# Linear attention in a sandwich kernel: the output projection multiplied into the heads' sums, queries divided before it, and two stages of a state-space block moved from PSUM to SBUF

## The chip, the core and the metric

The kernel runs on one core of a Trainium2 chip. The core has five engines with queues of their own: TensorE (PE: matmuls, with the loads of stationary operands listed as PEld), VectorE (DVE), ScalarE (ACT), GpSimd (POOL) and SyncE (SP), which here issues nearly all DMAs. Each works through its instructions in the order in which they were emitted, and waits on semaphores for what the others have produced. Matmuls write into PSUM; VectorE and ScalarE take the results from there. All data are fp32.

The metric is the device time of one launch in microseconds. Three runs of the kernel before gave 2832.69, 2833.66 and 2833.69 us: median 2833.66.

## The reference

4 sequences of 1024 tokens with 256 features go through four blocks in turn: an encoder of 4 layers, a LoRA mixture, a state-space (Mamba) block of 512 channels with 16 states each, and a mixture of 8 experts that take up to 320 tokens each. The change touches two places. In each encoder layer, with 16 heads of 16 features:

```python
qp = elu(q) + 1                      # tokens x heads x 16
kp = elu(k) + 1
kv   = einsum('bshd,bshm->bhmd', kp, v)      # per head, summed over the sequence
ksum = sum(kp, axis=1)
z    = 1 / (einsum('blhd,bhd->blh', qp, ksum) + 1e-6)
attn = einsum('blhd,bhmd,blh->blhm', qp, kv, z)
x = x + (attn.reshape(b, t, 256) @ Wo + bo)
```

In the state-space block, before the recurrence over time:

```python
xc = conv_b + sum_k xp[:, k:k+L, :] * conv_w[:, k]     # 4 taps
xc = silu(xc)
dt, Bm, Cm = split(xc @ W_x)
delta = softplus(dt @ W_dt + b_dt)
h = h * exp(delta * A) + delta * xc * Bm ;  y = sum over the states of h * Cm
```

## The kernel before

**Tiling.** Tokens are cut into 8 blocks of 512 (two to a sequence), and each block into four tiles of 128. One encoder layer on one block is a "unit": there are 32. The units of two sequences alternate in two lanes, and a unit's work is cut into steps: `a_norm`, `a_turn`, `a_query`, `a_keys`, `a_sums` (projections and the heads' sums), `b_heads`, `b_turn`, `b_out`, `b_turn2` (attention and its output), `f_up`, `f_down` (feed-forward), and after the last layer `c_*` (the LoRA mixture). The loop at the end of `layers` (L1648) runs over the units and places in each round the early steps of unit u+3, the sums of u+2, the attention of u+1 and the feed-forward of u side by side. Between these steps, `pump` (L1637) draws pieces of `stream`: for each block `front` (input projection, convolution, softplus), `scan` (the recurrence), `back` and `route`, and at the end the experts. What remains of `stream` after the last round follows without encoder work beside it.

**Order.** Nothing is emitted at once. Every call is recorded (`record`, L191) with its reads, its writes and a planned duration from small tables (L132 to L152: for instance `SCATTER`, the planned price of one scattering DMA on GpSimd, 1010). `order` (L289) then repeatedly picks the operation that can start first by the plan; of several, the one recorded first. So an edit moves instructions on all engines.

**Buffers.** A tag of a pool stands for a ring of equal tiles. A tile is given a slot when its first operation is picked, and within a tag slots are given in the order of recording (L302 to L306, L332 to L339): a tile cannot get a slot before the tile recorded ahead of it. Four rings matter here: `mm`, four PSUM tiles of 512 columns, which all products use except the heads' sums (`kv`), the scan's sums (`y`) and the scan's states (`h`, two tiles); `tok`, four tiles for token-major data; `qe`, two tiles of 512 columns; `hc`, nine tiles.

**Attention before the change.** `a_sums` adds up, for each half c of the features, kp^T against v and a column of ones, over both blocks of a sequence, in PSUM. After the second block VectorE multiplies by the head mask (zero outside the 16x16 blocks on the diagonal) into `kvm`, 17 columns per head, the last of which holds the sums of kp. `b_heads` (L751) multiplies each tile of 128 queries with `kvm`; VectorE adds the epsilon to the 17th columns, takes the reciprocal (`z`) and multiplies (`a`, a `tok` tile). `b_turn` transposes `a` on TensorE, eight 128x128 transposes, and ScalarE copies the result into an `hT` tile. `b_out` (L780) multiplies it with `wo` and adds to the residual `X`.

**State-space stages before the change.** In `front`, each of four channel groups has an input product in an `mm` tile `ps`. ScalarE copies it to `xi` and writes the last tap with the bias back into `ps`; VectorE adds the other three taps into `ps` (L1093), and ScalarE and VectorE take sigmoid and product from it. Later another product in an `mm` tile gives dt @ W_dt; ScalarE makes |x| and relu(x) of it (the latter back into the tile), then exp and log; VectorE and GpSimd correct the logarithm, VectorE adds the parts into the tile (L1141), ScalarE copies that to `du`, and VectorE multiplies by `xc`.

**The scan.** A group of four channel rows by two state halves gives eight tiles `hc` = h * C; when all four of a half are there, TensorE sums them over the states with `gsum` into `y` (`sums`, L1164). The sums of one group are recorded behind the first two products of the next.

Of the kernel before, what the change touches and what calls it, by code (L numbers as in the profile page):

```python
# [9 lines left out]
F32 = mybir.dt.float32  # L10
# [138 lines left out]
ISSUE, SCATTER, FIND = 350, 1010, 1500  # L149
# [237 lines left out]
def sandwich_kernel(ctx: ExitStack, tc: tile.TileContext, io: dict):  # L387
# [34 lines left out]
    nc.vector.memset(eps, LN_EPS)  # L422

# [118 lines left out]
    def layers(ctx: ExitStack):  # L542
# [28 lines left out]
        head_blocks = head_mask.rearrange("p (h m) -> p h m", m=HD)  # L571

# [142 lines left out]
        def a_sums(u):  # L715
            s, l, j = units[u]
            half = j % NB
            if half == 0:
                KV[s, l] = ps_kv.tile([P, NC_D, P + 1], F32, tag="kv", name="kv")
            acc, kv = KV[s, l], S[u].pop("kv")  # L720
            for c in range(NC_D):
                for i in range(NT):
                    nc.tensor.matmul(
                        acc[:, c, :],
                        kv[:, 0, i, c, 0:P],
                        kv[:, 1, i, c, :],
                        start=half == 0 and i == 0 and c == 0,
                        stop=half == NB - 1 and i == NT - 1 and c == NC_D - 1,
                        skip_group_check=True,
                    )  # L730
            if half == NB - 1:

                kvm = apool.tile([P, NC_D, HC, HD + 1], F32, tag="kvm", name="kvm")
                shape = [P, NC_D, HC, HD]
                nc.vector.tensor_tensor(
                    kvm[:, :, :, 0:HD],
                    acc[:, :, 0:P].rearrange("p c (h m) -> p c h m", h=HC),
                    head_blocks.unsqueeze(1).to_broadcast(shape),
                    ALU.mult,
                )  # L740
                nc.vector.tensor_tensor(
                    kvm[:, :, :, HD],
                    head_blocks[:, :, 0].unsqueeze(1).to_broadcast([P, NC_D, HC]),
                    acc[:, :, P : P + 1].to_broadcast([P, NC_D, HC]),
                    ALU.mult,
                )
                for k in range(NB):
                    S[u - k]["kvm"] = kvm


        def b_heads(u):  # L751
            j = units[u][2]
            qT, kvm = S[u].pop("qT"), S[u].pop("kvm")
            nc.gpsimd.tensor_tensor(X[j], X[j], over_tiles(weight(u)["ro"][:, 0, :]), ALU.add)
            a = tok("att")
            for i in range(NT):
                ps = mm([P, NC_D * HC, HD + 1], "psa")
                for c in range(NC_D):
                    nc.tensor.matmul(
                        ps[:, c * HC : (c + 1) * HC, :].rearrange("p h m -> p (h m)"),  # L760
                        qT[:, c, i * P : (i + 1) * P],
                        kvm[:, c, :, :].rearrange("p h m -> p (h m)"),
                        start=True,
                        stop=True,
                    )
                z = small.tile([P, NC_D * HC], F32, tag="z", name="z")
                nc.vector.tensor_scalar(z, ps[:, :, HD], ATTN_EPS, None, ALU.add)
                nc.vector.reciprocal(z, z)
                nc.vector.tensor_tensor(
                    a[:, i, :].rearrange("p (h m) -> p h m", m=HD),  # L770
                    ps[:, :, 0:HD],
                    z.unsqueeze(2).to_broadcast([P, NC_D * HC, HD]),
                    ALU.mult,
                )
            S[u]["a"] = a

        def b_turn(u):
            S[u]["aT"] = turn(S[u].pop("a"))

        def b_out(u):  # L780
            j = units[u][2]
            w, aT = weight(u), S[u].pop("aT")
            for pr in range(NT // 2):
                ps = mm([P, 2, D], "pso")
                for k in range(2):
                    i = 2 * pr + k
                    for c in range(NC_D):
                        nc.tensor.matmul(
                            ps[:, k, :],
                            aT[:, c, i * P : (i + 1) * P],  # L790
                            w["wo"][:, c, :],
# [243 lines left out]
        def front(j):  # L1035
# [43 lines left out]
            for db, ps in project(w_in[0]):  # L1079
# [4 lines left out]
                else:  # L1084
                    nc.gpsimd.tensor_copy(xi[:, 0:3], m["hist"][:, db, :])
                nc.scalar.copy(xi[:, 3 : TB + 3], ps)
                nc.scalar.activation(
                    ps, ps, AF.Identity, bias=mcol[:, db, M_CB : M_CB + 1], scale=w[:, 3:4]
# [3 lines left out]
                for k in range(3):  # L1092
                    nc.vector.scalar_tensor_tensor(  # L1093
                        ps, xi[:, k : k + TB], w[:, k : k + 1], ps, ALU.mult, ALU.add
                    )
                s = sigmoid(ps)
                nc.vector.tensor_tensor(xc[:, db, :], s, ps, ALU.mult)
# [26 lines left out]
            for db in range(NDB):  # L1124
# [10 lines left out]
                nc.scalar.activation(ps, ps, AF.Relu, bias=bdt)  # L1135
# [5 lines left out]
                nc.vector.tensor_tensor(ps, v1, ps, ALU.add)  # L1141
                nc.scalar.copy(du[:, 0, :], ps)
                nc.vector.tensor_tensor(du[:, 1, :], xc[:, db, :], ps, ALU.mult)
# [4 lines left out]
        def scan(j):  # L1148
# [12 lines left out]
            for db in range(NDB):  # L1161
# [13 lines left out]
                for r in range(GQ):  # L1175
# [6 lines left out]
                    for q in range(4):  # L1182
# [10 lines left out]
                        for k in range(NSH):  # L1193
# [12 lines left out]
                            hc = tiles[q, k] = spool.tile([P, TB], F32, tag="hc", name="hc", bufs=9)  # L1206
# [441 lines left out]
        for u in range(-3, len(units) + 4):  # L1648
# [28 lines left out]
            parts.append(lambda: load(u + 2, "wo", "ro"))  # L1677
# [125 lines left out]
```

## Time and profile before

| | us |
|---|---|
| median of three runs | 2833.66 |
| the profiled execution | 2831.64 |
| its span, first to last instruction | 2829.7 |
| TensorE busy | 2424.3 |
| VectorE busy | 1876.2 |
| ScalarE busy | 1550.4 |
| GpSimd busy | 1122.1 |
| mean granted TensorE clock | 0.925 |

All lines of code that the planner emits carry one line number, L203, so groups are told apart by engine, operation, tile names and shape. A row of the groups reads: line, engine, operation, output tile <- inputs, shapes and count; then busy time in all and the mean length of one in ns; then how long the engine had been idle just before these instructions, and which engine's write to which tile ended that wait. Names are those of the tiles in PSUM or SBUF, not of the variables: `wo<-` groups contain the output projection, `t` is several things (weights and transposed blocks of the state-space part, `du`, small columns of the normalisation). An fp32 matmul stands as two records, a transpose as one. Means include the overlap of one instruction with the next; busy time doesn't.

Most of the scans run beside the encoder: at the encoder's last matmul, at 2296.6 us, the rows of `hc` show that about five and a half of the eight scans are done. The rest, with most of the experts, fills the last 533 us.

### The profile page before, as it was taken

The page shows a single profiled execution, that of the slowest core. Times are in us where ns is not written, and L with a number is a line of the kernel's source. Part 1 is how long each engine was busy: PE and PEld are TensorE (multiplying, and loading weights), DVE is VectorE, ACT ScalarE, POOL GpSimd, SP SyncE. Part 2 cuts the span into 40 slices and gives each one's busy share as a digit, 9 for nine tenths or more (in the row PEclk, how much of TensorE's full clock was granted, in tenths as well). Part 3 has the DMA queues.
Part 4 walks back from the last instruction along what each step waited for, and adds up shares of the span by engine and source line. Part 5 has one row for each costly group of instructions (what it writes and reads, how often), then busy time and mean ns, then how long its engine had stood idle before and what let it go on. Part 6 is the DMA issues. An engine that isn't in the chain of part 4 may idle for free. (4 is left out here: it accounts for less than half of the span.)

```text
span 2829.7 us, 30664 instructions
## 1 busy us (share of the span) xinstructions
PE 2424.3 (86%) x9172; PEld 1440.9 (51%) x9172; DVE 1876.2 (66%) x4182; ACT 1550.4 (55%) x3213; POOL 1122.1 (40%) x878
## 2 busy tenths in 40 slices
PE   4979799999899999997989999986986875789776
PEld 2556466666556555555645556543543443334343
DVE  3231323244387778885458979987987995599896
ACT  4333543545665666554665666665664544666443
POOL 0100011022054445452235446544654572467663
PEclk8989899999999999998999999998997886899878
DMA  4011110122253344442244445545445343867652
GB/s 116 17 56 48 52 38 28 40 71 82 96 182 125 104 137 144 127 134 66 92 152 137 145 131 173 165 139 168 135 144 157 108 151 112 248 185 216 189 163 62
DMA packets 202221, 342.09 MB, mean 121 GB/s; under 512 B 32197, under 2 KB 79514, under 8 KB 198976
## 3 DMA queue, kind: packets, MB, share of 16 engines
q1 hardware_dynamic: 197760, 334.80, 38.2%
q0 software_dynamic: 4288, 5.27, 1.0%
q8 instruction: 74, 1.21, 0.2%
q14 instruction: 99, 0.81, 0.1%
HBM read 281.13 MB, written 59.92 MB: 121 GB/s over the span
## 5 line engine op out<-in xcount | busy, mean ns | idle before, releaser
L203 POOL TENSOR_TENSOR dbu<-dd,bc 128x512 f32<-128x512 f32 x512 | 657.7, 1321 | 485.8 <-DVE h L203 262.2
L203 ACT ACTIVATE h<-dd,A 128x512 f32<-128x512 f32 x512 | 346.1, 687 | 340.1 <-DVE hc L203 333.0
L203 PE MATMUL mm<-w,fT 128*128 128x256 f32 x2176 | 486.6, 381 | 5.9 <-ACT t L203 3.3
L203 PEld LDWEIGHTS mm<-w,fT 128*128 128x128 f32 x2176 | 410.4, 190 | 84.6 <-issue 16.0
L203 PE MATMUL y<-hc,gsum 128*32 128x512 f32 x1024 | 260.4, 647 | 114.3 <-DVE hc L203 104.6
L203 DVE TENSOR_TENSOR hc<-h,bc 128x512 f32<-128x512 f32 x512 | 343.0, 679 | 21.0 <-PE y L203 17.5
L203 DVE TENSOR_TENSOR_SCAN h<-h,last_h,dbu 128x512 f32<-128x512 f32 x256 | 322.3, 1277 | 39.0 <-ACT h L203 31.5
L203 DVE TENSOR_TENSOR_SCAN h<-h,dbu 128x512 f32<-128x512 f32 x256 | 306.1, 1218 | 33.1 <-ACT h L203 26.0
L203 POOL TENSOR_TENSOR X<-X,ro 128x1024 f32<-128x1024 f32 x64 | 150.3, 2354 | 420.4 <-ACT tok L203 388.2
L203 PE MATMUL mm<-hT,w1a 128*128 128x512 f32 (+1 forms) x576 | 268.4, 614 | 9.1 <-ACT hT L203 8.2
L203 PE MATMUL mm<-hT,w1b 128*128 128x512 f32 (+1 forms) x576 | 253.3, 592 | 9.8 <-DVE tok L203 8.5
L203 ACT ACTIVATE fT<-mm,cols 128x512 f32<-128x512 f32 x256 | 172.3, 680 | 128.8 <-PE mm L203 127.8
L203 PE MATMUL mm<-wkv,hT 128*128 128x512 f32 x512 | 228.7, 599 | 4.5 <-DVE xc L203 3.2
L203 PE MATMUL mm<-ident,tok 128*128 128x128 f32 x952 | 145.0, 298 | 90.4 <-ACT tok L203 84.6
L203 DVE TENSOR_TENSOR X<-X,mm 128x512 f32<-128x512 f32 x128 | 86.8, 680 | 189.1 <-PE mm L203 188.8
L203 PEld LDWEIGHTS mm<-ident,tok 128*128 128x128 f32 x952 | 116.1, 152 | 157.2 <-ACT tok L203 88.6
L203 PEld LDWEIGHTS mm<-hT,w1a 128*128 128x128 f32 x576 | 111.8, 204 | 142.4 <-issue 99.3
L203 PEld LDWEIGHTS mm<-hT,w1b 128*128 128x128 f32 x576 | 110.3, 195 | 140.8 <-issue 106.9
L203 ACT ACTIVATE tok<-X,nb,rs 128x256 f32<-128x256 f32 x288 | 149.3, 589 | 34.1 <-DVE nb L203 33.8
L203 PEld LDWEIGHTS y<-hc,gsum 128*32 128x32 f32 x1024 | 38.8, 111 | 243.6 <-DVE hc L203 166.2
L203 PEld LDWEIGHTS mm<-wkv,hT 128*128 128x128 f32 x512 | 97.5, 192 | 122.0 <-issue 105.1
L203 ACT ACTIVATE tok<-tok,nb,rs 128x256 f32<-128x256 f32 x252 | 131.1, 590 | 38.1 <-DVE nb L203 34.4
(184 smaller groups left out, 3710.9 us busy)
## 6 DMA issues: line engine op xcount, KB each, us to landing
dd<-dud SPq DMA_DIRECT2D x512, 256.0 KB
w<-in_w_dram SPq DMA_DIRECT2D x16, 1024.0 KB
dud<-t SPq DMA_DIRECT2D x32, 512.0 KB
tok<-in_x_dram SPq DMA_DIRECT2D x16, 512.0 KB
wkv<-in_wkv_dram SPq DMA_DIRECT2D x16, 512.0 KB
w1a<-in_w_dram SPq DMA_DIRECT2D x16, 512.0 KB
w1b<-in_w_dram SPq DMA_DIRECT2D x16, 512.0 KB
t<-in_w_in_dram SPq DMA_DIRECT2D x16, 512.0 KB
```

What stands on the lines that cost most here:

```text
L203: getattr(getattr(self.nc, engine), name)(*map(put, args), **{k: put(v) for k, v in kwargs.items()})
```

## The change

In the attention, `kvm` keeps only the masked sums (`a_fold`). A second tile, `den`, holds the sums of kp, spread over the 16 columns of their head. `a_fold2` transposes the masked sums, and `a_fold3` multiplies them by `wo` once per sequence and layer, which gives `kvo`, 256x256. `b_heads` multiplies `den` with the queries, so that each feature row holds its head's denominator for 512 tokens; ScalarE takes logarithm and exponential of minus that, and VectorE multiplies the queries by it in place. `b_out` multiplies the divided queries by `kvo`. `b_turn` and `att` are gone. The tiles of the fold and the divisors `z` take the ring `qe`; `den` and `kvo` have one buffer each. The loads of `wo` come one unit earlier.

In `front`, the convolution is added up in `xc` in SBUF, from the first tap on; softplus's positive part goes to a `qe` tile, and the sum goes straight into `du` without ScalarE's copy. The ring `hc` gets eight tiles, and the planned price of a scatter is 1700.

```diff
-ISSUE, SCATTER, FIND = 350, 1010, 1500
+ISSUE, SCATTER, FIND = 350, 1700, 1500
...
-            if half == NB - 1:
-                kvm = apool.tile([P, NC_D, HC, HD + 1], F32, tag="kvm", name="kvm")
...
+        def a_fold(u):
+            s, l, j = units[u]
+            if j % NB < NB - 1:
+                return
+            acc = KV.pop((s, l))
+            t = apool.tile([P, 2, NC_D, P], F32, tag="qe", name="kvm")
+            nc.vector.tensor_tensor(
+                t[:, 0], acc[:, :, 0:P], head_mask.unsqueeze(1).to_broadcast([P, NC_D, P]), ALU.mult
+            )
+            den = apool.tile([P, NC_D, P], F32, tag="den", name="den", bufs=1)
+            nc.vector.tensor_tensor(
+                den,
+                head_mask.unsqueeze(1).to_broadcast([P, NC_D, P]),
+                acc[:, :, P : P + 1].to_broadcast([P, NC_D, P]),
+                ALU.mult,
+            )
...
+        def a_fold2(u):
...
+            pt = mm([P, NC_D, P], "ptk")
+            for c in range(NC_D):
+                nc.tensor.transpose(pt[:, c, :], t[:, 0, c, :], ident)
+            nc.scalar.copy(t[:, 1], pt)
+        def a_fold3(u):
...
+            ps = mm([P, NC_D, D], "psm")
+            for c in range(NC_D):
+                nc.tensor.matmul(
+                    ps[:, c, :], t[:, 1, c, :], weight(u)["wo"][:, c, :], start=True, stop=True
                 )
+            kvo = apool.tile([P, NC_D, D], F32, tag="kvo", name="kvo", bufs=1)
+            nc.scalar.copy(kvo, ps)
...
         def b_heads(u):
...
-            a = tok("att")
-            for i in range(NT):
-                ps = mm([P, NC_D * HC, HD + 1], "psa")
...
-                z = small.tile([P, NC_D * HC], F32, tag="z", name="z")
-                nc.vector.tensor_scalar(z, ps[:, :, HD], ATTN_EPS, None, ALU.add)
-                nc.vector.reciprocal(z, z)
...
-        def b_turn(u):
-            S[u]["aT"] = turn(S[u].pop("a"))
+            for c in range(NC_D):
+                ps = mm([P, TB], "psa")
+                nc.tensor.matmul(ps, den[:, c, :], qT[:, c, :], start=True, stop=True)
+                z = apool.tile([P, TB], F32, tag="qe", name="z")
+                nc.scalar.activation(z, ps, AF.Ln, bias=attn_eps)
+                nc.scalar.activation(z, z, AF.Exp, scale=-1.0)
+                nc.vector.tensor_tensor(qT[:, c, :], qT[:, c, :], z, ALU.mult)
...
-                            aT[:, c, i * P : (i + 1) * P],
-                            w["wo"][:, c, :],
+                            qT[:, c, i * P : (i + 1) * P],
+                            kvo[:, c, :],
...
+                t = xc[:, db, :]
                 nc.scalar.activation(
-                    ps, ps, AF.Identity, bias=mcol[:, db, M_CB : M_CB + 1], scale=w[:, 3:4]
+                    t, ps, AF.Identity, bias=mcol[:, db, M_CB : M_CB + 1], scale=w[:, 3:4]
                 )
...
-                        ps, xi[:, k : k + TB], w[:, k : k + 1], ps, ALU.mult, ALU.add
+                        t, xi[:, k : k + TB], w[:, k : k + 1], t, ALU.mult, ALU.add
                     )
-                s = sigmoid(ps)
-                nc.vector.tensor_tensor(xc[:, db, :], s, ps, ALU.mult)
+                s = sigmoid(t)
+                nc.vector.tensor_tensor(t, s, t, ALU.mult)
...
-                nc.scalar.activation(ps, ps, AF.Relu, bias=bdt)
+                r = apool.tile([P, TB], F32, tag="qe", name="over")
+                nc.scalar.activation(r, ps, AF.Relu, bias=bdt)
...
-                nc.vector.tensor_tensor(ps, v1, ps, ALU.add)
-                nc.scalar.copy(du[:, 0, :], ps)
-                nc.vector.tensor_tensor(du[:, 1, :], xc[:, db, :], ps, ALU.mult)
+                nc.vector.tensor_tensor(e, v1, r, ALU.add)
+                nc.vector.tensor_tensor(lv, xc[:, db, :], e, ALU.mult)
...
-                            hc = tiles[q, k] = spool.tile([P, TB], F32, tag="hc", name="hc", bufs=9)
+                            hc = tiles[q, k] = spool.tile([P, TB], F32, tag="hc", name="hc", bufs=8)
...
             add(a_sums, u + 2)
+            add(a_fold, u + 2)
             add(f_up, u, 0)
+            add(a_fold2, u + 2)
...
             add(b_heads, u + 1)
             add(f_up, u, 1)
+            add(a_fold3, u + 2)
...
-            add(b_turn, u + 1)
...
-            parts.append(lambda: load(u + 2, "wo", "ro"))
+            parts.append(lambda: load(u + 3, "wo"))
+            parts.append(lambda: load(u + 2, "ro"))
```

More of the change, by code (lines that the diff above doesn't have):

```diff
@@ L422, in sandwich_kernel @@
     nc.vector.memset(eps, LN_EPS)
+    attn_eps = cpool.tile([P, 1], F32, name="attn_eps")
+    nc.vector.memset(attn_eps, ATTN_EPS)
     nc = Program(tc)
@@ L570, in layers @@
                 units += [st and (st[0], st[1], st[0] * NB + k) for k in range(NB)]
-        head_blocks = head_mask.rearrange("p (h m) -> p h m", m=HD)
         W = {}
@@ L730, in a_sums @@
                     )
-            if half == NB - 1:
-                kvm = apool.tile([P, NC_D, HC, HD + 1], F32, tag="kvm", name="kvm")
[L734 to L739, printed above, removed]
-                )
[L741 to L748, printed above, removed]
+        def a_fold(u):
[14 more added lines that the diff above has]
+            )
+            S[u]["fold"] = t
+            for k in range(NB):
+                S[u - k]["den"] = den
@@ new lines, in a_fold2 @@
+        def a_fold2(u):
+            if "fold" not in S[u]:
+                return
+            t = S[u]["fold"]
+            pt = mm([P, NC_D, P], "ptk")
[3 more added lines that the diff above has]
+        def a_fold3(u):
+            if "fold" not in S[u]:
+                return
+            t = S[u].pop("fold")
+            ps = mm([P, NC_D, D], "psm")
+            for c in range(NC_D):
+                nc.tensor.matmul(
+                    ps[:, c, :], t[:, 1, c, :], weight(u)["wo"][:, c, :], start=True, stop=True
+                )
+            kvo = apool.tile([P, NC_D, D], F32, tag="kvo", name="kvo", bufs=1)
+            nc.scalar.copy(kvo, ps)
+            for k in range(NB):
+                S[u - k]["kvo"] = kvo
@@ L751, in b_heads @@
         def b_heads(u):
             j = units[u][2]
-            qT, kvm = S[u].pop("qT"), S[u].pop("kvm")
+            qT, den = S[u]["qT"], S[u].pop("den")
             nc.gpsimd.tensor_tensor(X[j], X[j], over_tiles(weight(u)["ro"][:, 0, :]), ALU.add)
-            a = tok("att")
-            for i in range(NT):
-                ps = mm([P, NC_D * HC, HD + 1], "psa")
[L758 to L765, printed above, removed]
-                z = small.tile([P, NC_D * HC], F32, tag="z", name="z")
-                nc.vector.tensor_scalar(z, ps[:, :, HD], ATTN_EPS, None, ALU.add)
-                nc.vector.reciprocal(z, z)
[L769 to L774, printed above, removed]
@@ L775, in b_heads @@
-            S[u]["a"] = a
-        def b_turn(u):
-            S[u]["aT"] = turn(S[u].pop("a"))
+            for c in range(NC_D):
[5 more added lines that the diff above has]
+                nc.vector.tensor_tensor(qT[:, c, :], qT[:, c, :], z, ALU.mult)
@@ L780, in b_out @@
         def b_out(u):
             j = units[u][2]
-            w, aT = weight(u), S[u].pop("aT")
+            w, qT, kvo = weight(u), S[u].pop("qT"), S[u].pop("kvo")
             for pr in range(NT // 2):
```

## The prediction

> **What bounds the kernel now.** I read the page's first parts, then busy times by stretch, then the groups of instructions kept apart by shape, with what ended the idle time before each. First the totals and the share of each fortieth of the span in tenths, from the page:
>
> ```profile
> PE 2424.3 (86%) x9172; PEld 1440.9 (51%) x9172; DVE 1876.2 (66%) x4182; ACT 1550.4 (55%) x3213; POOL 1122.1 (40%) x878
> ...
> PE   4979799999899999997989999986986875789776
> ...
> DVE  3231323244387778885458979987987995599896
> ```
>
> TensorE (PE) is near nine tenths for two thirds of the span; VectorE (DVE) joins it later. Busy times by stretch (length, then busy us and counts of PE, PEld, DVE, ACT, POOL, then granted clock, DMA share, GB/s):
>
> ```profile
> 0.00:700.00 700.00, 612.82 (x2312) 402.21 (x2313) 222.55 (x715) 317.06 (x717) 77.10 (x53) 0.94 0.18 54
> 700.00:1900.00 1200.00, 1107.68 (x4366) 668.96 (x4364) 894.90 (x1995) 739.40 (x1504) 538.29 (x423) 0.97 0.43 133
> 1900.00:2297.00 397.00, 310.81 (x1141) 169.63 (x1140) 340.94 (x666) 220.83 (x404) 218.94 (x175) 0.87 0.45 140
> 2297.00:2830.00 533.00, 393.04 (x1360) 200.10 (x1356) 417.82 (x808) 273.14 (x589) 287.77 (x229) 0.84 0.56 167
> ```
>
> The reader should see two regimes. Until 1900 TensorE is the bound: 613 of 700 us, then 1108 of 1200 us (92%), with VectorE at 32% and 75%. The last down-projection of the encoder ends at 2296.6 us in the timeline. Around it, from 1900, VectorE leads (341 of 397 us). The last 533 us are the remaining scans and the experts, which the change hardly touches. So what is taken from TensorE counts in the first two stretches. Third, the groups that the change removes, and idle time on TensorE ("idle" is before the group, with what ended it):
>
> ```profile
> L203 DVE TENSOR_TENSOR hc<-h,bc 128x512 f32<-128x512 f32 x512 | 343.0, 679 | 21.0 <-PE y L203 17.5 <-DMA bc<-bcd 1.6 <-DVE t L203 0.3
> ...
> L203 PE MATMUL mm<-hT,w1b 128*128 128x512 f32 x512 | 234.6, 612 | 9.8 <-DVE tok L203 8.5 <-ACT fT L203 1.2
> ...
> L203 PE MATMUL mm<-ident,tok 128*128 128x128 f32 x952 | 145.0, 298 | 90.4 <-ACT tok L203 84.6 <-DVE tok L203 2.8 <-DVE kv L203 1.7
> ...
> L203 PE MATMUL mm<-hT,wq 128*128 128x512 f32 x256 | 121.2, 618 | 4.7 <-ACT hT L203 3.5 <-DVE X L203 1.2
> L203 PE MATMUL mm<-wo,hT 128*128 128x256 f32 x512 | 118.8, 385 | 1.1 <-ACT hT L203 1.1
> ...
> L203 PE MATMUL mm<-kvm,qT 128*128 128x136 f32 x512 | 82.7, 311 | 40.7 <-ACT t L203 14.6 <-DVE tok L203 7.5 <-ACT fT L203 7.4
> ...
> L203 ACT ACTIVATE qe<-mm,nbq 128x512 f32<-128x512 f32 x64 | 43.4, 679 | 44.9 <-PE mm L203 44.2
> ...
> L203 ACT COPY hT<-mm 128x512 f32<-128x512 f32 x64 | 34.3, 584 | 23.3 <-PE mm L203 23.3
> ```
>
> A matmul that waits for a DVE or ACT instruction it takes no data from waits for one of the four PSUM tiles "mm": the heads' product (mm<-kvm,qT) waited 14.6 us for "ACT t", the copy that ends a softplus, and 7.5 us for "DVE tok", the division of the previous token tile.
>
> **What the Trainium skill says.** "Perfetto Trace Analysis", Optimization Strategy, says that repeating gaps on the engine that should be saturated can mean that no SBUF or PSUM buffer was free; the 14.6 us above agree. The same page, Optimizing Scalar/DVE Operations, prices a ScalarE access at about 93 ns in SBUF and 51 in PSUM, a VectorE access at 60 and 125. For ScalarE the trace agrees: the exponential of the sigmoid is 592 ns from PSUM and 630 from SBUF. For VectorE it doesn't show it: 128x512 products with a PSUM operand take 679 to 687 ns, one wholly in SBUF (tok with affine, 692). "VectorE: DVE Perf Modes", Why tensor_tensor can't do 2×_2P or 4×, leaves fp32 two-tensor operations no fast mode, and 692 ns for 512 columns agrees. So the convolution gains nothing per instruction by leaving PSUM.
>
> **The change part by part.** There are 32 units (block and layer) in 16 pairs. An fp32 matmul stands as two records, a transpose as one; I price by a group's busy time over its count, in which overlap is already taken out.
>
> 1. TensorE. Removed: the heads' products, 82.7 us, and the turning of their result, 8 transposes a unit, 256 of the 952 of "ident,tok": 256/952 x 145.0 = 39.0. Sum 121.7. Added: denominators, two 128x512 matmuls a unit, 128 records x 121.2/256 (row of wq) = 60.6; fold per pair two transposes, 32 x 145.0/952 = 4.9, and two 128x256 matmuls, 64 records x 118.8/512 (row of wo) = 14.8. Sum 80.3. The output projection keeps its shape and count. Net -41.4 us, 1.29 a unit.
> How much counts? The heads' products lie 192, 256 and 64 of 512 in the first three stretches: 12, 16 and 4 units, worth 15.5, 20.7 and 5.2 us. I take 0.95, 0.85 and 0.6 of these, by how far TensorE is the bound there: 14.7 + 17.6 + 3.1 = -35.4. Bounds: 0 where another engine takes over everywhere, -41.4.
>
> 2. VectorE. Removed: the three z groups (89.8 us in the view of tile z) and two masks (8.5). Added: the queries' division, 64 products of 128x512 at 680 ns = 43.5, and two 256-column masks a pair, 32 x 424 ns = 13.6. Net -41.2. That is what lets step 1 count where VectorE is nearly as busy; it isn't added again.
>
> 3. ScalarE. Removed: copies of the turned heads, 34.3, and the copy of delta into "du", 32 x 582 ns = 18.6. Added: logarithms, 64 x 679 (qe<-mm above) = 43.5; exponentials, 64 x 625 (qe<-qe in the same view) = 40.0; fold copies, 16 x (377 for 256 columns + 584 for 512) = 15.4. Net +46.0, 1.44 a unit. ScalarE is busy 739 of 1200 us in the second stretch, so most of it lies beside TensorE; but the scan waits for its exponential ("DVE h" for "ACT h", 57.5 us in the table of waits), and a queue in order gets later. I take +6 (a tenth of that). Bounds 0 and 20 units x 1.44 = +29.
>
> 4. PSUM freed at once. A convolution tile was held over two ScalarE and three VectorE operations, a sigmoid and a product; now over two ScalarE operations. A softplus tile was held over two GpSimd operations as well. The heads take two tiles a unit for one logarithm each, where four were held by VectorE, and their turn took two more. Idle ended by these releases: heads 14.6 + 7.5, w1b 8.5 (DVE tok), and from rows of the view not shown, input projection 3.5 and keys 3.2 (DVE xc), experts' transposes 9.4 (DVE t): 46.7 us. Some of it comes back as waiting for data. I take half, -23.4; bounds 0 and -46.7.
>
> 5. Ring "hc" from 9 to 8. One group of eight products fills it; the next group's first product must wait until the sums on TensorE have read the former. One element's time of slack is lost, 1.23 + 0.68 = 1.9 us. Now 17.5 of 21.0 us idle before hc are for "PE y". I take +8, near half as much again; bounds 0 and the slower rival below.
>
> 6. Buffers and queues. "qe" (two buffers) now also holds the folded sums, the divisors and softplus's positive part; queries stay until the output projection; "att" no longer takes a "tok" buffer or an "hT". The weights wo are fetched one unit earlier, since only the fold reads them: on SP's queue the scans' loads stand behind that fetch, and what it waits for now comes earlier. Net 0, plus or minus 8. The larger price of a scatter alters only the planned order on GpSimd. Its DMAs keep their count, 28 at 1012 and 24 at 1543 ns: 0, plus or minus 5. Start-up: from the mask at 71.8 to the first output projection at 77.1 us is 5.3 us; mask 0.85, matmul 1.0, logarithm, exponential and product for two chunks come to about as much: 0. In the tail, front's chain loses little: -1.
>
> Set side by side, both instruction orders have 5.6 of the 8 scans' sums on TensorE ahead of the last encoder matmul, so no scan work moves into the tail.
>
> Sum: -35.4 + 6 - 23.4 + 8 - 1 = -45.8 us. The profiled execution took 2831.64 us (span 2829.7 and 1.9 around it), 2.0 under the median 2833.66. Forecast on the median: 2833.66 - 45.8 = 2788 us.
>
> **The rivals.**
> A. The work goes but little time does: VectorE or ScalarE take over, and PSUM waits turn into data waits. For: VectorE is at 86 to 96 in several 100 us windows from 800 on. Against: VectorE loses 41 us too. Half of step 1 (-18), none of step 4, +14 of steps 3 and 5 is -4; with half of that cost -11. Say 2824.
> B. PSUM pays in full and the tail gains: -41 - 47 + 8 = -80, 2754. For: removing "att" also frees tok and hT buffers. Against: VectorE bounds from 1900.
> C. Slower: the hc ring. It acts at each of 63 joins between groups, and costs up to 1.9 us each. It decides from 46/63 = 0.73 us a join on the path. At 1.2 us: 63 x 1.2 = 76, less 46: +30, 2864. For: 13 such waits exist with nine buffers, up to 4.1 us long, and the tail's expert matmuls run up to 15 us without a break (in the chain of waits), with VectorE at 96% there. Against: 47 of the joins lie before the tail, where TensorE is mostly the bound, and VectorE can run two scans ahead into the two "h" banks.
> That the program doesn't do what it says is excluded: the counts of instructions differ exactly by those of steps 1 to 3.
>
> **How the numbers follow.** Main case 0.64, own range 2768 to 2810; A 0.16; B 0.08; C 0.12. About 0.2%, 5.7 us, is what a measurement of this kernel can tell from no change. A splits 0.11 faster and 0.05 same; C 0.02 same and 0.10 slower. Faster 0.83, same 0.07, slower 0.10. The range leaves out the far half of B and C: 2757 to 2832. The unknown bounds of steps 3 to 5 fit in it.
>
> **What would show it.** Step 1: about 2383 us busy on TensorE, the heads' product at 60 us; the last down-projection 35 to 50 us earlier than 2297. Steps 2, 3: VectorE about 1835, ScalarE about 1596. Step 4: no matmul of the heads, w1b or keys waits for "ACT t", "DVE xc" or "DVE tok". Step 5: idle before hc for "PE y" near 26 us; over 60 speaks for C. I am wrong if the encoder's end moves by less than 20 us (A), or if the tail after it grows beyond 533 us by more than 15 (C).

## The result, and the profile after

| | before | after |
|---|---|---|
| median, us | 2833.66 (5 runs, 2831.52 to 2835.67) | 2820.14 (5 runs, 2813.88 to 2822.18) |
| ratio to before, 95% interval | | 0.995 (0.9936 to 0.9965) |
| the profiled execution / its span, us | 2831.64 / 2829.7 | 2818.76 / 2817.0 |
| end of the encoder's last down-projection, us | 2296.6 | 2277.5 |
| what follows it, us | 533.1 | 539.5 |
| mean granted TensorE clock | 0.925 | 0.921 |

The change gains 13.5 us, 0.5%. The forecast was 45.8. First the totals and the fortieths of the page of the changed kernel:

```profile
PE 2416.0 (86%) x8628; PEld 1386.3 (49%) x8628; DVE 1894.9 (67%) x3863; ACT 1586.0 (56%) x3277; POOL 1149.9 (41%) x878
...
PE   4879799999999999997989998986986975789776
...
DVE  3121323244397778886468899997998995699885
```

TensorE is busy 8.3 us less (2424.3 before), where 41.4 had been priced. VectorE has 319 instructions fewer and is still busy 18.7 us *more* (1876.2 before), where 41.2 us less had been priced: a miss of 60 us. ScalarE rose by 35.6 (46.0 priced). GpSimd, whose instructions the change leaves alone, is busy 27.8 us more (1122.1 before). The stretches, with the columns as before (length, then busy us and counts of PE, PEld, DVE, ACT, POOL, granted clock, DMA share, GB/s); the last one ends with the span, at 2817:

```profile
0.00:700.00 700.00, 608.30 (x2114) 381.63 (x2115) 207.83 (x597) 337.04 (x753) 77.58 (x53) 0.94 0.17 55
700.00:1900.00 1200.00, 1104.57 (x4111) 640.97 (x4110) 932.62 (x1855) 763.38 (x1550) 560.87 (x429) 0.97 0.42 133
1900.00:2297.00 397.00, 320.42 (x1107) 169.38 (x1106) 348.90 (x644) 222.01 (x408) 226.44 (x173) 0.85 0.46 144
2297.00:2817.00 520.00, 382.69 (x1301) 194.28 (x1299) 405.58 (x771) 263.58 (x567) 284.97 (x224) 0.83 0.56 167
```

Before 700 us VectorE falls by 14.7 us (222.55 to 207.83), as it should. From 700 to 1900 us it is at 932.62 (894.90 before), 78% of the stretch. The groups that the change adds or alters show why both engines came out dearer (busy us, mean ns, then idle before the group and what ended it):

```profile
L203 DVE TENSOR_TENSOR hc<-h,bc 128x512 f32<-128x512 f32 x512 | 342.6, 678 | 16.2 <-PE y L203 14.5
...
L203 PE MATMUL mm<-hT,w1b 128*128 128x512 f32 x512 | 230.7, 601 | 5.0 <-ACT fT L203 3.4 <-ACT qe L203 1.3
...
L203 PE MATMUL mm<-kvo,qT 128*128 128x256 f32 x512 | 119.3, 385 | 2.8 <-ACT kvo L203 2.5
L203 PE MATMUL mm<-ident,tok 128*128 128x128 f32 x696 | 114.8, 304 | 106.2 <-ACT tok L203 93.7 <-DVE kv L203 9.9 <-ACT hT L203 0.9
...
L203 DVE SCALAR_TENSOR_TENSOR xc<-xi,mcol,xc 128x512 f32<-128x512 f32 x96 | 81.1, 845 | 39.2 <-ACT xc L203 31.4 <-ACT xi L203 4.8 <-ACT r L203 2.3
...
L203 PE MATMUL mm<-qT,den 128*128 128x512 f32 x128 | 68.8, 657 | 9.4 <-ACT qe L203 6.1 <-ACT fT L203 3.1
...
L203 DVE TENSOR_TENSOR qT<-qT,qe 128x512 f32<-128x512 f32 x64 | 54.0, 852 | 76.9 <-ACT qe L203 76.7
...
L203 DVE TENSOR_TENSOR t<-xc,t 128x512 f32<-128x512 f32 x32 | 39.1, 1222 | 0.8
...
L203 DVE TENSOR_TENSOR t<-sg,qe 128x512 f32<-128x512 f32 x32 | 33.8, 1056 | 22.5 <-POOL sg L203 20.3 <-POOL kv L203 2.1
...
L203 DVE TENSOR_TENSOR xc<-sg,xc 128x512 f32<-128x512 f32 x32 | 26.2, 819 | 21.0 <-ACT sg L203 20.9
...
L203 PE MATMUL mm<-wo,qe 128*128 128x256 f32 x64 | 17.9, 404 | 1.8 <-ACT qe L203 1.8
...
L203 PE MATMUL mm<-ident,qe 128*128 128x128 f32 x64 | 13.1, 305 | 8.3 <-DVE rs L203 3.6 <-ACT fT L203 2.4 <-DVE qe L203 1.6
```

Three things are to be seen. The output projection (mm<-kvo,qT) costs what it did (119.3 us, 118.8 before), the denominators (mm<-qT,den) 68.8 instead of the 60.6 priced. The turning of the heads took only 145.0 - 114.8 = 30.2 us with it, not 39.0. And the five VectorE groups whose operands all lie in SBUF now take 819 to 1222 ns apiece in the mean. Before, with one operand in PSUM, the convolution's taps took 746 and the three others 681 to 687; the queries' product is new and had been priced at 680. Taps 81.1 instead of 71.6, the other three 99.1 instead of 65.6, and the queries' product 54.0 instead of 43.5: 53.5 us of the 60.

**TensorE's price.** The same place of the encoder on TensorE's timeline (start, us in all, operation, count), before:

```profile
454.56 2.37 PE L203 MATMUL mm<-kvm,qT 128*128 128x136 f32 x16
456.82 7.13 PE L203 MATMUL mm<-hT,w1b 128*128 128x512 f32 x16
463.79 1.91 PE L203 MATMUL mm<-ident,tok 128*128 128x128 f32 x16
465.53 2.76 PE L203 MATMUL mm<-w,fT 128*128 128x256 f32 x12
```

and after:

```profile
453.90 1.88 PE L203 MATMUL mm<-qT,den 128*128 128x512 f32 x4
455.62 4.88 PE L203 MATMUL mm<-hT,w1b 128*128 128x512 f32 x11
```

Taken from start to start, a unit's head products occupy TensorE for 456.82 - 454.56 = 2.26 us (2.58 priced), its half of the 16 turns 1.74 / 2 = 0.87 (1.22 priced), and its denominators here 455.62 - 453.90 = 1.72; in the units beside which a fold lies it is 2.05, in the mean 1.88 (1.89 priced). Where TensorE is saturated (390 to 590 us: 197.5 of 200 us busy, granted clock 1.00) the end of one unit's down-projection follows the other so:

| unit | before | after |
|---|---|---|
| 6 | 437.63 | 436.97 |
| 7 | 486.40 | 484.22 |
| 8 | 535.18 | 532.98 |
| 9 | 583.94 | 580.23 |

Before, 48.77 us a unit. After, 47.25 and 48.76 in turn, the longer one with a fold in it: 1.53 us less a pair, 0.77 a unit instead of 1.29. The starts agree roughly: 2.26 + 0.87 - 1.88 = 1.25 a unit, less the fold's own products and transposes, which take 0.86 + 0.22 us a pair from start to start and so 0.54 a unit, leaves 0.71. Over 32 units 0.77 is 24.5 us, not 41.4.

Why the price was too high, the same row of the kernel before says, first from 390 to 590 us and then from 1900 to 2297:

```profile
L203 PE MATMUL mm<-kvm,qT 128*128 128x136 f32 x64 | 9.1, 286 | 0.4
```

```profile
L203 PE MATMUL mm<-kvm,qT 128*128 128x136 f32 x64 | 13.5, 372 | 20.1 <-ACT t L203 14.6 <-DVE t L203 4.4 <-DVE tok L203 1.1
```

Each stretch holds four units. Where TensorE has no gaps, the row itself gives 9.1 / 4 = 2.28 us a unit, all but the 2.26 from start to start. The 2.58 is the mean over the whole span, with the 3.38 us a unit from 1900 on, where the granted clock is 0.87 and the products wait between each other. For the turns the row gives 0.98 in the first stretch (96 records, 11.8 us), so there 0.24 of the miss of 0.35 comes of the stretch and 0.11 of overlap. How far the clock and how far the waits raise the mean was not separated.

**VectorE behind GpSimd.** The lengths of two of the slow groups in the changed kernel (minimum/median/maximum in ns), and below them the same two operations in the kernel before:

```profile
L203 DVE TENSOR_TENSOR t<-sg,qe x32: 673/692/2831, 776.6 to 2600.9; 128x512 f32<-128x512 f32 x32
L203 DVE TENSOR_TENSOR t<-xc,t x32: 667/693/2736, 777.8 to 2602.7; 128x512 f32<-128x512 f32 x32
```

```profile
L203 DVE TENSOR_TENSOR mm<-sg,mm x32: 669/688/697, 781.2 to 2612.2; 128x512 f32<-128x512 f32 x32
L203 DVE TENSOR_TENSOR t<-xc,mm x32: 649/686/689, 782.2 to 2614.0; 128x512 f32<-128x512 f32 x32
```

The median is the old price; some instructions take up to four times as long, and before none did. Two excerpts of the timeline of all engines show when. In the first, GpSimd has begun:

```profile
785.06 2.35 POOL L203 TENSOR_TENSOR X<-X,ro 128x1024 f32<-128x1024 f32 x1
785.13 2.83 DVE L203 TENSOR_TENSOR t<-sg,qe 128x512 f32<-128x512 f32 x1 [1.16 <-POOL sg L203]
787.99 0.69 ACT L203 ACTIVATE qe<-mm,nbq 128x512 f32<-128x512 f32 x1 [2.46 <-DVE t L203]
787.99 0.69 DVE L203 TENSOR_TENSOR t<-xc,t 128x512 f32<-128x512 f32 x1
```

GpSimd's residual sum runs from 785.06 to 787.41. VectorE's addition starts 0.07 us later and ends at 787.96, 0.55 us after GpSimd's; the next one of its kind, with GpSimd idle, takes 0.69. ScalarE's next operation stood still 2.46 us for it, since the addition held a tile of the ring "qe". In the second, VectorE has begun:

```profile
1007.54 0.67 DVE L203 TENSOR_TENSOR t<-xc,t 128x512 f32<-128x512 f32 x1
...
1007.70 1.63 POOL L203 TENSOR_TENSOR dbu<-dd,bc 128x512 f32<-128x512 f32 x1 [1.77 <-DVE h L203]
...
1009.32 0.67 DVE L203 TENSOR_TENSOR qT<-qT,qe 128x512 f32<-128x512 f32 x1
...
1009.54 1.58 POOL L203 TENSOR_TENSOR dbu<-dd,bc 128x512 f32<-128x512 f32 x1 [0.21 <-POOL dbu L203]
```

Now the two VectorE operations take 0.67, and GpSimd's products 1.63 and 1.58 us, where such a product takes 1.28 alone. So whichever starts second waits for the other. The two excerpts are no exceptions. Of the 256 instructions of the five groups 73 begin while GpSimd is in a two-operand sum or product that lasts at least another 0.12 us, and 71 of these end 0.55 us behind it; 65 of the 68 that take over 0.8 us are among the 73. In the kernel before, 58 of the 192 instructions of the four old groups begin in that way, and none of the 192 takes over 0.76 us. The Trainium skill, "SBUF — State Buffer", section "SBUF: two separate sides", states just this: VectorE and GpSimd share a pair of ports as an exclusive lock, held for the whole instruction, which a VectorE operation with two SBUF inputs takes against a GpSimd operation that reads SBUF. This trace agrees. The prediction didn't use that page.

### The profile page after: what moved, and what is told of

Its sections match the earlier page's. It is cut to its first block, busy times and chain, and to the rows that moved or that the text cites. A ratio compares the mean times of both kernels' runs of the same rounds, so it can differ in the third digit from the quotient of the medians.

```text
span 2817.0 us, 29326 instructions
## 1 busy us (share of the span) xinstructions
PE 2416.0 (86%) x8628; PEld 1386.3 (49%) x8628; DVE 1894.9 (67%) x3863; ACT 1586.0 (56%) x3277; POOL 1149.9 (41%) x878
## 4 chain that ended last, share of the span: by engine, by line
DVE 22%; PE 22%; ACT 8%; issue 6%; POOL 4%; DMA 2%; SPq 0%; DVEq 0%; POOLq 0%; ACTq 0%
PE mm L203 18%; DVE h L203 8%; DVE hc L203 4%; ACT tok L203 3%; PE y L203 3%; DVE t L203 2%; POOL dbu L203 2%; DVE st L203 2%; ACT h L203 1%; DVE xc L203 1%; PE kv L203 1%; ACT qe L203 1%; POOL sg L203 1%; DVE kv L203 1%; POOL tok L203 1%
## 5 line engine op out<-in xcount | busy, mean ns | idle before, releaser
L203 POOL TENSOR_TENSOR dbu<-dd,bc 128x512 f32<-128x512 f32 x512 | 672.6, 1344 | 479.1 <-DVE h L203 265.5
L203 DVE TENSOR_TENSOR hc<-h,bc 128x512 f32<-128x512 f32 x512 | 342.6, 678 | 16.2 <-PE y L203 14.5
L203 PE MATMUL mm<-hT,w1a 128*128 128x512 f32 (+1 forms) x576 | 266.2, 611 | 11.8 <-ACT hT L203 10.6
L203 PE MATMUL mm<-ident,tok 128*128 128x128 f32 x696 | 114.8, 304 | 106.2 <-ACT tok L203 93.7
L203 PEld LDWEIGHTS mm<-ident,tok 128*128 128x128 f32 x696 | 86.5, 154 | 164.5 <-ACT tok L203 95.6
```

The costliest lines, as they stand in the source:

```text
L203: getattr(getattr(self.nc, engine), name)(*map(put, args), **{k: put(v) for k, v in kwargs.items()})
```

## The experiments

Each run is compared with the kernel before on the same chip; ratios have 95% intervals. "Encoder's end" is the last down-projection in the run's timeline.

**The two halves apart.** `fold_only` is the new kernel with convolution and softplus as before; `front_only` is the kernel before with those two stages as after, and so with nine `hc` tiles and the scatter's price of 1010, where `fold_only` has eight and 1700. Both edits are these lines, in opposite directions:

```diff
-                t = xc[:, db, :]
...
-                    t, ps, AF.Identity, ...
+                    ps, ps, AF.Identity, ...
...
-                        t, xi[:, k : k + TB], w[:, k : k + 1], t, ALU.mult, ALU.add
+                        ps, xi[:, k : k + TB], w[:, k : k + 1], ps, ALU.mult, ALU.add
...
-                s = sigmoid(t)
-                nc.vector.tensor_tensor(t, s, t, ALU.mult)
+                s = sigmoid(ps)
+                nc.vector.tensor_tensor(xc[:, db, :], s, ps, ALU.mult)
...
-                r = apool.tile([P, TB], F32, tag="qe", name="over")
-                nc.scalar.activation(r, ps, AF.Relu, bias=bdt)
+                nc.scalar.activation(ps, ps, AF.Relu, bias=bdt)
...
-                nc.vector.tensor_tensor(e, v1, r, ALU.add)
-                nc.vector.tensor_tensor(lv, xc[:, db, :], e, ALU.mult)
+                nc.vector.tensor_tensor(ps, v1, ps, ALU.add)
+                nc.scalar.copy(du[:, 0, :], ps)
+                nc.vector.tensor_tensor(du[:, 1, :], xc[:, db, :], ps, ALU.mult)
```

> The changed kernel with convolution and softplus put back in PSUM; fold, ring hc of 8 and scatter price stay. Theory T1 (VectorE instructions whose two big inputs both lie in SBUF stand still while GpSimd works; in the changed kernel that took back about 53 us of VectorE time: convolution taps 746 to 845 ns, softplus sum 687 to 1056, delta times xc 682 to 1222): VectorE busy about 1852, ratio to before 0.985 to 0.992, faster than the changed kernel (0.995). Rival T2 (holding PSUM tiles long is what costs, so leaving PSUM is the better half of the change): ratio 0.998 or more, slower than the changed kernel. Rival T3 (the ring of 8 takes the gain back): same as the changed kernel, 0.995.

> The kernel before with only convolution and softplus moved out of PSUM (softplus's positive part in a qe tile); attention, ring of 9 and scatter price as before. T1: VectorE busy about 1876 + 43 = 1919, ratio 1.000 to 1.008. T2 (PSUM freed early pays): 0.990 to 0.997. T3 says nothing of it but that the ring isn't touched: 0.995 or less.

Measured: the fold alone 2830.12 us, 1.000 (0.9991 to 1.0009); the front alone 2824.00, 0.9974 (0.9964 to 0.9985). Together they gain 13.5 us, apart 0 and 7. Both miss what T1, the theory of the two SBUF operands, expected (0.992 or less for the fold, 1.000 or more for the front): it had the lengths right and not the times. That the fold alone gains nothing, where TensorE's part should be 24.5 us shorter, needed a cause of its own.

**The divisors in PSUM.** `z_psum` is the new kernel with logarithm and exponential in place in the product's PSUM tile; the queries' product then has one operand in PSUM, and "qe" is free of divisors. `fold_z_psum` is the same with convolution and softplus as before.

```diff
-                z = apool.tile([P, TB], F32, tag="qe", name="z")
-                nc.scalar.activation(z, ps, AF.Ln, bias=attn_eps)
-                nc.scalar.activation(z, z, AF.Exp, scale=-1.0)
-                nc.vector.tensor_tensor(qT[:, c, :], qT[:, c, :], z, ALU.mult)
+                nc.scalar.activation(ps, ps, AF.Ln, bias=attn_eps)
+                nc.scalar.activation(ps, ps, AF.Exp, scale=-1.0)
+                nc.vector.tensor_tensor(qT[:, c, :], qT[:, c, :], ps, ALU.mult)
```

> The changed kernel with the divisor's logarithm and exponential written back into the PSUM tile, so that the queries' product has one input in PSUM. T1: the product falls from 852 to about 685 ns in the mean and from 1805 to under 760 at most, VectorE busy 10 us less, ratio to before 0.990 to 0.994. T2: two PSUM tiles are held over three operations instead of one, so TensorE waits more: 0.996 to 1.002.

> The fold with divisors in PSUM, and convolution and softplus in PSUM as before: no new VectorE instruction with two big SBUF inputs. T1: VectorE busy about 1842, the best of the four, ratio to before 0.981 to 0.990. T2: the worst of the four that have the fold, 0.998 or more. T3: 0.995 like the changed kernel.

Measured: `z_psum` 2821.77, 0.9969 (0.9957 to 0.9981), no better than the changed kernel; `fold_z_psum` 2809.32, 0.9922 (0.9911 to 0.9934), 20.8 us below `fold_only`. It is the best of the four, as T1 had it, but short of T1's 0.990. The row of the queries' product in `z_psum`:

```profile
L203 DVE TENSOR_TENSOR qT<-qT,mm 128x512 f32<-128x512 f32 x64 | 42.5, 680 | 67.5 <-ACT mm L203 67.5
```

680 ns instead of 852, from the one operand that moved to PSUM. That saves 11.5 us of VectorE, and it is not where the 20.8 us come from, as the next runs show.

**The ring "qe".** The fold's tile `t` is held from the mask to the last product of the fold, several steps of the round, and takes one of only two "qe" tiles. `fold_t_hT` (from `fold_only`) and `after_t_hT` (from the changed kernel) move it to another ring and leave the divisors in "qe":

```diff
-            t = apool.tile([P, 2, NC_D, P], F32, tag="qe", name="kvm")
+            t = apool.tile([P, 2, NC_D, P], F32, tag="hT", name="kvm")
```

> The run fold_only (ratio 1.000; divisors in the SBUF ring qe) with the fold's own tile, which is held from the mask to the fold's last matmul, moved from the ring qe to the ring hT, which the turned heads no longer use. Theory Q (the long hold leaves the divisors one buffer, so the two halves of the heads follow each other and TensorE waits): 0.992 to 0.996, and the fifth unit's down-projection ends 3 us or more ahead of before, as it does with divisors in PSUM. Theory T1 (the queries' product with two SBUF inputs stands behind GpSimd): unchanged, 0.999 to 1.001, since GpSimd is nearly idle there and the product stays in SBUF.

> The changed kernel with one word altered: the fold's own tile stands in the ring hT instead of qe. Theory Q (the hold in qe blocks divisors, queries' exponentials and softplus's part behind it): the gains of the parts then add up, fold_t_hT -21 us and front_only -7 us, so about 2803 us, ratio 0.988 to 0.992, and the encoder ends 25 to 32 us before that of the kernel before. If the ring is not what ate the changed kernel's gain: 0.994 to 0.997, the encoder's end at 19 us as now.

Measured: `fold_t_hT` 2810.02, 0.9925 (0.9911 to 0.9938), the whole 20.1 us with the queries' product still in SBUF; its encoder's end is 2269.5 us, against 2292.1 in `fold_only`. `after_t_hT` is 2813.48, 0.9936 (0.9924 to 0.9949), its encoder's end 2277.0: the parts' gains were to add up to 0.988 to 0.992, and beside the new front the ring's relief cannot be told from none. `after_zp_t_hT` does both edits on the changed kernel:

> As the last one, and the divisors in PSUM. Theory Q alone: the same time as the last one within 0.2%, since ring qe is free in both. Theory T1 (VectorE standing behind GpSimd in the queries' product costs time): 5 us or more faster than the last one.

Measured: 2820.84, 0.9963 (0.9952 to 0.9975), again no gain over the changed kernel. So the two buffers of "qe" are what holds the fold back when it comes alone: two different edits that relieve them gain the same 20 us. Something else holds it back in the full change.

**The ring "hc".** `before_hc8` is the kernel before with

```diff
-                            hc = tiles[q, k] = spool.tile([P, TB], F32, tag="hc", name="hc", bufs=9)
+                            hc = tiles[q, k] = spool.tile([P, TB], F32, tag="hc", name="hc", bufs=8)
```

> The kernel before with the ring hc cut from 9 to 8. Prediction's step 5: about +8 us (ratio 1.003), idle before hc for PE y from 17.5 to about 26 us. Theory R (the ring is what ate the gain): +20 us or more, 1.007. Theory T4 (the gain was mis-sized: TensorE's short groups were priced with the fill of its pipeline in them, 1.29 us a unit where the saturated stretch shows 0.77): the ring costs next to nothing, 0.998 to 1.003.

Measured: 2844.12, 1.0052 (1.0038 to 1.0066), some 14 us slower where +8 had been priced. The row that was to show it:

```profile
L203 DVE TENSOR_TENSOR hc<-h,bc 128x512 f32<-128x512 f32 x512 | 342.6, 680 | 18.4 <-PE y L203 16.9
```

Idle for "PE y" is 16.9 us, not 26 (17.5 with nine tiles). The time stands in another place than that row: the encoder's end is 5.2 us later and the tail 540.4 instead of 533.1 us. In the changed kernel the row says 14.5, and its tail is 539.5. Which wait carries the 14 us was not found, and they come from one order of instructions, where another order alone moves the time by up to 10 us (next).

**How much is the order.** Nearly any edit reorders all engines. `HANDOVER` is a price of the planner (36); another value changes the order and no instruction. `before_plan` and `after_plan` set it to 40, and `after_sc1010` puts the price of a scatter back:

```diff
-HANDOVER = 36
+HANDOVER = 40
...
-ISSUE, SCATTER, FIND = 350, 1700, 1500
+ISSUE, SCATTER, FIND = 350, 1010, 1500
```

> The kernel before with one planning constant altered, the handover between engines 40 instead of 36: the same instructions in a somewhat different order. It measures how far an order alone moves the time. If the order is worth little, 0.999 to 1.001; if the differences of 10 to 20 us between the variants of the fold are of the order's making, this one moves by 5 us or more, either way.

> The changed kernel with the handover constant 40 instead of 36. The kernel before moved by -10 us with it, the fold with divisors in PSUM by -9. If that is a gain of the constant itself, about 2810 us, 0.9925; if it is the scatter of orders, anything from 0.992 to 0.998.

> The changed kernel with the planned price of a scatter back at 1010. Only the planned order from the first scatter on can differ (about the fourteenth unit). Prediction's step 6: within 5 us of the changed kernel, ratio 0.993 to 0.998. If the scatter price was what carried the change's gain: 0.998 or more.

Measured: `before_plan` 0.9965 (0.9951 to 0.9978), `after_plan` 0.9971 (0.9961 to 0.9982), `after_sc1010` 0.9963 (0.9951 to 0.9976). The kernel before is 10 us faster with the very same instructions. The repeatability of one order is far better than what a change of order does; a difference between single variants below some 0.3% can't be laid to an edit. That takes away any verdict on the scatter's price.

**The square in three orders.** To get under this, four corners were run at three values of `HANDOVER`: the kernel before, the front alone, the fold alone, and both. In the two with the fold the divisors lie in PSUM, so that the fold's hold on the ring "qe" doesn't mix in; these two also keep eight `hc` tiles and the scatter's 1700. What these runs were to show:

> The best run so far (fold with divisors in PSUM, ratio 0.9922) with the handover constant 40 instead of 36. If its gain is that of the fold (24.6 us of TensorE time by the saturated stretch, 0.9913), 0.990 to 0.995. If it came from a lucky order, 0.996 to 1.000.

> Only convolution and softplus out of PSUM, handover 40. Theory T1 (their two-SBUF-input instructions stand behind GpSimd where VectorE is the bound): mean of the three orders 0.998 to 1.001, no gain on the yardstick. Theory T2 (freed PSUM pays): 0.994 or less.

> Fold with divisors in PSUM and convolution and softplus out of PSUM, handover 40. T1: mean of three orders 0.995 to 0.998, that is 0.003 to 0.006 behind the fold alone. If the difference seen so far (0.9969 against 0.9922) is an order's accident: within 0.001 of the fold alone in the mean.

> The kernel before in a third order (handover constant 32). Between 0.996 and 1.002; the mean of its three orders (1.000, 0.9965 and this) is the yardstick of the square, about 0.9985.

> Only convolution and softplus out of PSUM, handover 32. Theory T1: mean of the three orders no better than that of the kernel before (0.998 to 1.001). Theory T2 (freed PSUM pays): mean 0.994 or less.

> Fold with divisors in PSUM and convolution and softplus out of PSUM, handover 32. T1: mean of three orders 0.995 to 0.998, 0.003 to 0.006 behind the fold alone. If only orders differ: within 0.001 of the fold alone in the mean.

> Fold with divisors in PSUM alone, handover 32. The other two orders gave 0.9922 and 0.9892; by TensorE's 0.77 us a unit, 24.6 us, and the ring's cost, 0.989 to 0.993.

Measured, ratio to the kernel before:

| corner | 36 | 40 | 32 | mean |
|---|---|---|---|---|
| before | 1 | 0.9965 | 0.9987 | 0.9984 |
| front alone (`front_only`, `front_p40`, `front_p32`) | 0.9974 | 0.9979 | 0.9970 | 0.9974 |
| fold alone (`fold_z_psum`, `foldz_plan`, `foldz_p32`) | 0.9922 | 0.9892 | 0.9897 | 0.9904 |
| both (`z_psum`, `zpsum_p40`, `zpsum_p32`) | 0.9969 | 0.9968 | 0.9944 | 0.9960 |

The fold gains 0.80%, 22.7 us, its ring of eight and its scatter price included. Taking convolution and softplus out of PSUM gains 0.1% without the fold, which isn't resolved, and *costs* 0.56%, 16 us, with it. All three orders agree on that sign. So the two halves work against each other as they stand. Since the ring of eight comes with the fold, and the front was not run with eight tiles but no fold, the ring may have its part in this. Means over the profiled execution of each of the three orders, as ends of a unit's down-projection against those of before:

| us | front alone | fold alone | both |
|---|---|---|---|
| unit 20 (at 1296.5 before) | -1.9 | -20.8 | -21.2 |
| unit 26 (at 1749.3) | +1.9 | -21.4 | -25.4 |
| unit 32 (at 2296.6) | -1.3 | -24.6 | -12.8 |

Up to unit 26 both together are 4.0 us ahead of the fold alone; at the end of the last six units they are 11.8 us behind it. That is the part in which VectorE leads. Its groups there (from 1725 to 2285 us), in `fold_z_psum`:

```profile
L203 DVE SCALAR_TENSOR_TENSOR mm<-xi,mcol,mm 128x512 f32<-128x512 f32 x24 | 17.8, 743 | 3.9 <-ACT mm L203 3.9
...
L203 DVE TENSOR_TENSOR mm<-sg,mm 128x512 f32<-128x512 f32 x8 | 5.5, 689 | 0.0
L203 DVE TENSOR_TENSOR t<-xc,mm 128x512 f32<-128x512 f32 x8 | 5.5, 687 | 3.9 <-ACT t L203 3.6
...
L203 DVE TENSOR_TENSOR xc<-sg,mm 128x512 f32<-128x512 f32 x8 | 5.4, 680 | 1.2 <-ACT sg L203 1.2
```

and in the changed kernel:

```profile
L203 DVE SCALAR_TENSOR_TENSOR xc<-xi,mcol,xc 128x512 f32<-128x512 f32 x24 | 22.5, 937 | 4.8 <-ACT xc L203 4.8
...
L203 DVE TENSOR_TENSOR t<-xc,t 128x512 f32<-128x512 f32 x8 | 11.3, 1413 | 0.2
...
L203 DVE TENSOR_TENSOR t<-sg,qe 128x512 f32<-128x512 f32 x8 | 9.7, 1213 | 8.5 <-POOL sg L203 8.5
...
L203 DVE TENSOR_TENSOR xc<-sg,xc 128x512 f32<-128x512 f32 x8 | 7.9, 988 | 0.2 <-ACT sg L203 0.2
```

The same 48 operations take 34.2 us and 51.4: 17 us more of the engine that is busiest there (500.85 of 560 us in the changed kernel, 483.67 in `fold_z_psum`), near the 16 us that both together lose against the fold alone from unit 26 to unit 32, and the 16 us lost in all. `z_psum` shows 50.2 us for the same rows, so these lengths are the front's doing, not the divisors'. In `front_only` they take 46.0 us and yet the encoder's end doesn't move. That the fold, by shortening TensorE's part, makes VectorE's time count is the likeliest reason; it was argued, not isolated.

**The granted clock.** One more thing goes along with these times and was not held apart. In the three orders (36, 40, 32) the mean granted clock of an execution has medians of 0.918, 0.917 and 0.9195 with both halves, and of 0.9235, 0.9225 and 0.924 with the fold alone; the kernel before has 0.923. `fold_only` and the changed kernel have 0.919, `fold_t_hT` 0.922. Among the executions of one kernel the slower ones mostly show the lower clock: `fold_t_hT` took 2802.11 us at 0.926 and 2809.39 to 2810.87 at 0.922, `z_psum` 2812.65 at 0.923 and 2818.26 to 2825.04 at 0.916 to 0.920. A line through all executions of the square, each kernel taken against its own mean, gives 1.1 us for 0.001. By this estimate between 5 and 6 of the 16 us, and some 3 to 5 of the 20 us laid to the ring "qe", go with the clock. Whether these edits lower the clock or only met it, the runs don't show.

**The best version.** The fold with divisors in PSUM, front as before and `HANDOVER` 40 (`foldz_plan`) takes 2800.04 us, 0.9892 (0.9877 to 0.9908), faster than both kernels. Its page:

```profile
PE 2411.1 (86%) x8628; PEld 1388.2 (50%) x8628; DVE 1824.0 (65%) x3863; ACT 1590.3 (57%) x3309; POOL 1119.6 (40%) x878
```

VectorE is at 1824.0 us, near what step 2 had forecast for the change (1835).

## Why the prediction was right in direction and wrong in size

**Step 1 failed by its price.** Busy time over count, taken over the whole span, gave 1.29 us a unit; the saturated stretch shows 0.77. The heads' products (2.26 instead of 2.58) and the turns (0.87 instead of 1.22) are nearly all of the miss: their means hold the records of stretches in which TensorE waits or has a lower clock, and for the turns some overlap. With 0.77 the full step is 24.5 us. The encoder's end moved by 24.6 us in the fold's corner over three orders, so about the whole of it arrived there, more than the shares of 0.95, 0.85 and 0.6 that were taken; how much of this the freed PSUM tiles of step 4 brought was not separated.

**Step 2 failed by its rule.** "So the convolution gains nothing per instruction by leaving PSUM" was true of the undisturbed instruction (medians 692 and 693 ns), and was read as "it costs nothing". Two SBUF operands put it behind GpSimd. VectorE did not fall by 41.2 us, it rose by 18.7. The front, which brings most of this, costs 16 us beside the fold, clock and ring of eight not held apart. The row taken as proof, the product wholly in SBUF (tok with affine, 692 ns), was a poor sample: its four instructions start between 2813.7 and 2818.1 us, where GpSimd has no instruction left in the kernel before (its last sum starts at 2801.94, its last DMA at 2804.31). Where a row lies in the span belongs to its price.

**Step 3** had ScalarE at 1596; it is 1586.0. Its cost of 6 us was not measured apart.

**Step 4 was right on the waits and wrong on their worth.** The heads' products no longer wait for "ACT t" or "DVE tok" (qT,den: 9.4 us idle, of which "ACT qe" 6.1), and w1b no longer for "DVE tok". But 23.4 us had been put on it, and the front alone, which frees most of these tiles, gains 0.1% in the mean of three orders. The bound of nothing, given in that step, was the better value. The 14.6 us, the largest item, are two waits of 7.3 us each, at 1940 and 2154 us; with the keys' 3.2, the input projections' 3.5, the experts' 9.4 and 1.1 of the heads' 7.5 some 32 of the 46.7 us lie after 1900, where the prediction itself had VectorE in the lead. Some idle time came back elsewhere: before "ident,tok" it is 106.2 us (90.4 before), before the keys 9.4 (4.5), 7.6 of it for "DVE qT".

**Step 5** was of the right sign and, by one order, too small: 14 us where eight buffers are tried alone, 8 priced, and not by the wait that had been named. So rival C's waits at the joins did not appear (16.9 us for "PE y", 17.5 before), and its size didn't either: the tail grew by 6.4 us, not by more than 15.

**Step 6** put the buffers at nothing, plus or minus 8. The fold's tile in "qe" costs 20 us without the new front, and in the full change nothing that these runs resolve.

**The sum.** On the means of three orders the fold with its eight `hc` tiles and divisors in PSUM gives -22.7, and the front beside it +16, together -7. The single pair of orders that was compared gave -13.5, since the order of before is 0.16% above its own mean and that of after, at 0.995 against 0.9961 over its three (`after`, `after_plan`, `after_sc1010`), below it. Rival A had the right shape: the encoder's end moved by 19.1 us, under the 20 named as its mark, and the time is 4 us from its 2824. That the number is so near is luck in part: A took half of step 1's 35.4 for the fold (the saturated stretch gives 24.5 for the full step), and had no lengthening of VectorE's instructions. Its reason, VectorE taking over, fits the last units, and there VectorE's own instructions became longer; that this is what makes it the bound was argued, not isolated.

## What to carry to other kernels

Price a TensorE group that goes or comes in a stretch where TensorE has no gaps, by the distance from its first start to the start of what follows, and not by its mean over a span in which it also waits. See in which stretch a wait lies before its end is counted as a gain. Before moving a VectorE operand from PSUM to SBUF, look at what GpSimd runs beside it: here an instruction with two SBUF inputs waited out whole GpSimd instructions. When an edit reorders everything, run each version in several orders before believing a difference of a few tenths of a per cent, note the granted clock of each, and cross the parts: two halves measured together hid a gain of 0.80% behind a loss of 0.56%.

## What the hardware showed that was not expected

A VectorE operation of 0.69 us took 2.83 us beside a GpSimd operation of 2.35 us, and GpSimd's 1.28 us product took 1.63 us when VectorE had begun first. The wait stands in the profile as busy time, so VectorE's share rises and no row names a wait; only minimum, median and maximum of a group betray it. With one operand in PSUM the same operations beside GpSimd kept to 0.76 us and less. And the same instructions in another order differed by 0.35%, where the interval of one order against another is 0.13% to either side.
